# The bias of a graph network's C projection in 64x64 tiles, and a new order of the period

## The chip, the cores and the metric

The kernel runs on one core of one Trainium2 chip. The core has five engines that work side by side, each with an instruction queue of its own that it executes in order: PE (TensorE, matmuls), DVE (VectorE), ACT (ScalarE), POOL (GpSimd) and SP (which only issues DMAs here). The metric is the device time of one execution in microseconds (us). Before the change three runs took 699.24, 699.70 and 699.98 us; the median is 699.7.

## What is computed

There are 128 graphs of 128 nodes with 64 features (x), each with a dense 128x128 matrix adj, about 6% of it nonzero. Two layers follow each other, each with a residual and a normalisation over the features.

```python
# layer 0, per graph: mask = adj > 0
h   = relu((x @ W1a)[j] + (x[j] - x[k]) @ W1b + b1)    # for every pair j, k; 192 wide
hm  = sum over k of h * mask[j, k]
x   = layernorm(x + hm @ W2 + deg[j] * b2)             # deg[j] = number of neighbours of j
# layer 1, per graph
agg = adj @ x
out = elu(elu(agg @ V1 + c1) @ V2 + c2) @ V3 + c3
x   = layernorm(x + out)
```

The pair sum is not computed densely. For each node j the kernel gathers only the rows of its neighbours: h[j, k] = relu(A[j] + C[k]) with A = x @ (W1a + W1b) + b1 and C = -x @ W1b. The sum of relu is taken from the sum of absolute values, since relu(t) = (t + |t|) / 2, and the linear half is put right by a correction (corr). The term deg[j] * b2 comes for free if every neighbour's row of C carries b2 in 64 extra columns: C has 192 + 64 = 256 columns, and the last 64 are multiplied by the mask itself, not by the relu.

## The kernel before

**Work.** Two graphs make a pair; there are 64 pairs, and the steady state is one pair per period. In a pair the nodes are sorted by degree and laid into nine blocks (BLOCKS), each with a number of neighbour slots. Block i of a pair is a "unit": ACT copies A into a PSUM bank (L955, here called acopy i), PE adds the neighbours' C rows by 18 matmuls against one-hot matrices (L966, gather i), and DVE sums absolute values over the slots (L976, sum i). Three PSUM banks (e0 to e2) rotate among the units, so acopy of a unit waits for the sum of the unit three before it. C is held as three bf16 parts (cf, rest, low) whose sum is the f32 value; each gather takes all three.

**The threads of a pair.** prepare counts degrees (mk, L576), spreads them on PE (L263, tiles identb and degb), ranks them (cmp, L597) and makes the permutation (perm, L605). sort_x sorts x, projects A (L632, L636), makes aj and later ea, sa and corr. sort_mask sorts the mask and makes the nine one-hot matrices (oh, L707). turn transposes adj and x. project_c makes C (L741), adds the bias in a step of its own, and splits the result. finish makes hm, multiplies by W2, returns to the node order (unsort), normalises, and does layer 1 (aggregate, hidden1, hidden2, last), up to the store. Five more PSUM banks (m0 to m4) serve all these steps; a step takes the bank that was given back first, and so waits for whoever read it last.

**The bias before.** b2 is split into three bf16 parts too. A 128x64 tile b2p is zero except in rows 0, 32 and 64, which hold the parts (copied there by POOL, L393), so that a matmul of a 128-row matrix of ones with b2p adds the sum of the parts to every row. The step is named bias in project_c, with 128x64 tiles (mode "t"), between the projection in 64x64 tiles (mode "r", L741) and the copy cf (L756).

**Order.** Nothing is ordered by hardware waits alone. A small planner (class Flow) writes the instructions into the queues. Every thread is a list of steps, each with an engine, a planned cost and the events it needs, and DUE gives each step a due time relative to its pair's start, ROUND (11.1651) apart. Until the first gather is laid, the planner takes the step that its planned clocks say is ready first. From then on (under_way) it takes, of all steps whose inputs are laid already, the one with the smallest due time. LAST shifts the dues of the last six pairs' finish threads, and pairs from LATE = NP - 2 on do more of finish on DVE and ACT. The overflow test (L858 to L879) near the end finds rows with too many neighbours for their block; none are found for these inputs, and a slow path behind it isn't run.

**Constants.** consts_b2 loads and splits b2 on POOL (helper parts, L389 to L393); scratch tiles hi, hm (as rest), mid and low are shared with the later split of c3's row (consts_late). consts_slots, on POOL, ends with memsets, one of them for b2p.

Of the kernel before, what the change touches and what calls it, by code (L numbers as in the profile page):

```python
# [31 lines left out]
F32 = mybir.dt.float32  # L32
# [3 lines left out]
OP = mybir.AluOpType  # L36
# [150 lines left out]
def sparse(tc, env):  # L187

    g = type("env", (), dict(env))
    nc, P, N, F, H, O, HB, H1, NP, E = (  # L190
        g.nc, g.P, g.N, g.F, g.H, g.O, g.HB, g.H1, g.NP, g.E)
# [11 lines left out]
    AHEAD = 4  # L203

    DUE = {
        "prepare": (-21.4113, -21.4103, -20.8009, -20.0167, -16.5154),
        "sort_x": (-11.5423, -11.5413, -2.7266, -2.3845, 0.0214, 1.3277, 2.8168, 12.6347),
        "sort_mask": (-10.347, -9.218, -8.7754, -8.3524, -5.8935, -5.758, -5.757, -5.756,
            -5.755, -5.754, -5.1217, -5.1207, 1.0998, 1.1008),
        "turn": (-26.2816, -24.1632),  # L210
        "project_c": (-13.6709, -12.5698, -12.2977, -12.2751, -11.3882, -10.0036, -8.4866),
        "finish": (13.0404, 22.189, 23.0263, 23.6287, 24.5439, 27.278, 28.4137, 32.117, 34.5413,
            35.4475, 35.4637, 36.1308, 36.1318, 36.1328, 37.7091, 43.35, 43.6764, 45.3519,
            45.5256, 46.0637, 48.8402, 49.096, 49.261, 51.6959, 51.9284),
        "unit": [(-1.48, -0.1838, 0.7496), (0.1062, 0.9216, 0.9226), (0.3987, 1.0968, 1.978),
            (1.1956, 1.4908, 2.221), (2.1682, 2.6234, 3.9141), (2.1874, 3.6496, 4.2699),
            (2.4467, 4.3465, 5.2271), (8.5772, 9.7062, 10.187), (5.7368, 9.4611, 10.7836)],
        "consts_late": (14.79, 24.13, 25.63, 26.63, 26.78, 26.79, 26.8, 26.81, 26.82, 27.82,
            28.82, 29.82, 30.82, 31.82, 32.82, 33.82, 34.82, 35.82, 36.82, 37.82, 38.82, 39.82,
            40.82),  # L220
    }

    LATE = NP - 2
    LAST = ((-3.5, -9.4, -4.9, -1.3), (5.5, -4.3, 0.3, 7.6), (-0.9, -2.8, 3.8, 7.6), (0.1, -0.2, -0.4, 5.1), (0.0, -1.6, 0.0, 0.2), (0.0, 0.0, 0.2, 0.0))

    def begin_thread(name, p, gen):
        due = DUE[name]
# [30 lines left out]
    HALVES = (slice(0, P // 2), slice(P // 2, P))  # L258

    def tiled(out, lhsT, rhs, **kw):  # L260

        for h in HALVES:
            nc.tensor.matmul(out[h], lhsT[:, h], rhs, **kw)  # L263
# [9 lines left out]
    const, temp = g.const, g.const  # L273
# [12 lines left out]
    ident = const([P, P], F32, "ident")  # L286
    identb = const([P, P], BF16, "identb")
    onesb = const([P, 2 * P], BF16, "onesb")
# [19 lines left out]
    wc = const([P, H + O], F32, "wc")  # L308
# [10 lines left out]

    b2r = const([P, O], F32, "b2r")  # L320
    b2p = const([P, O], BF16, "b2p")
    NR = 2 * O
    rows = temp([P, NR], F32, "rows")
    rowp = const([P, NR], BF16, "rowp")
# [15 lines left out]
    def made(*names):  # L340
        return [event("const", name) for name in names]

    def op(engine, cost, fn, name, *after):

        ev, = yield (engine, cost, made(*after), 0, fn)
        happened(ev, "const", name)
# [39 lines left out]
    def parts(row, to, n):  # L386

        hi, rest, mid, low = (t[:, :n] for t in scratch)
        return [("hi", lambda e: e.tensor_copy(hi, row)),  # L389
                ("rest", lambda e: e.tensor_sub(rest, row, hi)),  # L390
                ("mid", lambda e: e.tensor_copy(mid, rest)),
                ("low", lambda e: e.tensor_sub(low, rest, mid))] + [
                    (f"{i}", lambda e, i=i, t=t: e.tensor_copy(to[32 * i:32 * i + 1, :],  # L393
                                                               t[32 * i:32 * i + 1, :]))
                    for i, t in enumerate((hi, mid, low))]
# [18 lines left out]
    def consts_slots():  # L414
        v = nc.gpsimd
        iota = dict(allow_small_or_imprecise_dtypes=True)
        for i, (base, n, p0, p1, s) in enumerate(LAY):
            yield from op("POOL", 0.45, lambda: v.iota(
                slotc[:, base:base + n], pattern=[[2, s], [0, p1 - p0]], base=1,
                channel_multiplier=0, **iota), "slotc" if i == NB - 1 else f"slotc{i}")  # L420

        def scale():
            for p0, p1, s in BLOCKS:
                v.memset(srow[:, :, p0:p1], float(s))
        yield from op("POOL", 1.0, scale, "srow")
        yield from op("POOL", 0.2, lambda: v.memset(b2p, 0.0), "b2p0")
        for s in range(2):
            yield from op("POOL", 0.3, lambda: v.memset(v1p[:, s], 0.0), f"v1p0{s}")

# [64 lines left out]
        yield from op("DVE", 0.3, blocks, "wad", "wa", "wab0")  # L494

    def consts_b2():
        last = ["b2", "b2p0"]
        for name, fn in parts(b2r, b2p, O):
            yield from op("POOL", 0.25, lambda: fn(nc.gpsimd), "b2" + name, *last)
            last = ["b2" + name]  # L500
        happened(event("const", "b22"), "const", "b2p")

    def consts_banks():

# [227 lines left out]
    def project_c(p, ev):  # L732

        d = S[p]
        cols = H + O

        def project(*cps):
            for s in range(2):
                k = slice(s * F, (s + 1) * F)
                for h in HALVES:  # L740
                    nc.tensor.matmul(cps[s][h, :cols], d["turned"][k, 2, h], wc[k, :],  # L741
                                     start=True, stop=False)
        ev, *cps = yield ("PE:r", 0.43, [ev] + made("wc"), 2, project)

        def bias():
            for s in range(2):
                tiled(cps[s][:, H:cols], onesb[:, :P], b2p, start=False, stop=True)
        ev, = yield ("PE:t", 0.06, [ev] + made("b2p", "onesb"), 0, bias)
        cf = prep.tile([P, 2, cols], F32, name="cf", bufs=6)
        rest = prep.tile([P, 2, cols], F32, name="rest", bufs=6)  # L750
        low = prep.tile([P, 2, cols], BF16, name="low", bufs=6)
        d["cp"] = lambda i, s, c: low[:, s, c] if i == 2 else upper((cf, rest)[i][:, s, :])[:, c]
        hi = []
        for s in range(2):
            e, = yield ("ACT", act(cols), [ev], 0,
                        lambda: nc.scalar.copy(cf[:, s, :], cps[s][:, :cols]))  # L756
            hi.append(e)
        for s in range(2):
            ev, = yield ("DVE", dve(cols), [hi[s]], 0,
                         lambda: nc.vector.tensor_sub(rest[:, s, :], cps[s][:, :cols],  # L760
                                                      upper(cf[:, s, :])))
            flow.give(cps[s], ev)
        ev, = yield ("POOL PORT", 1.12, [ev], 0,
                     lambda: nc.gpsimd.tensor_sub(flat(low), flat(rest), upper(flat(rest))))  # L764
        happened(ev, "cp", p)
# [468 lines left out]
```

## Time and profile before

| | us |
|---|---|
| median of three runs | 699.7 (699.24 to 699.98) |
| the profiled execution itself | 699.37 |
| its span, first to last instruction | 697.6 |
| PE busy | 676.6 (97%) |
| DVE busy | 674.2 (97%) |
| ACT busy | 621.2 (89%) |
| POOL busy | 583.4 (84%) |
| gathers, L966, three groups | 210.9, 209.0, 209.0 |
| sums, L976 | 336.8 |
| one-hot compares, L707 | 155.9 |

A busy share counts the time in which the engine has at least one instruction under way; PE's matmuls overlap and their ends are modelled, so for PE the distance from one start to the next says more than the duration. In timeline lines the first number is the start in us after the span's start, the second the duration of all that the line merges ("x4": four instructions), then engine, line of the kernel, operation, output<-inputs by tile names, and shapes. PEld is the weight load of PE. In the groups, a number after the bar is busy time and mean ns of one. Windows give each engine's busy time in a stretch, then the granted clock of PE, the DMA share and GB/s.

### The profile page before, as it was taken

To read this page: it belongs to the slowest core of one execution; us is meant where nothing else is said; L and a number is where in the kernel's file an instruction comes from. 1 tells how busy PE (TensorE), PEld (TensorE's weight loads), DVE (VectorE), ACT (ScalarE), POOL (GpSimd) and SP (SyncE) were. 2 spreads that over 40 slices of the span, in tenths; PEclk is the share of its full clock that TensorE was granted. 3 is DMA by queue.
4 is the path that set the end of the run, shared out by engine and by line. 5 is a ranking of instruction groups with operands and counts; after the bars stand their busy time and mean duration, and the time that the engine had idled before them with its cause. 6 is when DMAs were issued, how large, how long until landed. Compare 5 with 4: busy or idle time off the path is not lost.

```text
span 697.6 us, 40860 instructions
## 1 busy us (share of the span) xinstructions
PE 676.6 (97%) x17245; PEld 610.3 (87%) x17246; DVE 674.2 (97%) x2267; ACT 621.2 (89%) x1731; POOL 583.4 (84%) x983
## 2 busy tenths in 40 slices
PE   7989999999999999999999999999999999999984
PEld 4878999999999999999999999999999999989972
DVE  6899999999999999999999999999999999999985
ACT  3678999999999999999999999999999999999963
POOL 5447988988988898898899889899888888899873
PEclk9999999999999999999999999999999999999996
DMA  3200111110110111111011011101101101100000
GB/s 93 56 3 3 35 26 27 35 34 19 34 34 19 33 34 26 27 34 34 19 35 33 23 31 34 32 20 34 34 19 33 34 23 30 35 22 9 12 9 20
DMA packets 54988, 20.01 MB, mean 29 GB/s; under 512 B 37904, under 2 KB 54800, under 8 KB 54800
## 3 DMA queue, kind: packets, MB, share of 16 engines
q1 hardware_dynamic: 54096, 17.06, 10.1%
q8 instruction: 137, 2.24, 1.3%
q14 instruction: 51, 0.42, 0.2%
q10 hardware_dynamic: 704, 0.30, 0.2%
HBM read 13.14 MB, written 4.19 MB: 25 GB/s over the span
## 4 chain that ended last, share of the span: by engine, by line
PE 90%; DVE 4%; POOL 2%; ACT 2%; issue 1%; DMA 1%; SPq 0%; POOLq 0%; DVEq 0%; ACTq 0%
PE e L966 46%; PE m L263 23%; PE m L741 4%; PE m L636 3%; PE m L722 3%; PE m L917 2%; PE m L619 2%; PE m L632 2%; DVE sums L976 1%; PE m L657 1%; PE m L661 1%; PE m L723 1%; POOL rs L787 1%; ACT e L955 1%; DVE oh L707 1%
## 5 line engine op out<-in xcount | busy, mean ns | idle before, releaser
L955 ACT COPY e<-aj 128x504 f32<-128x504 f32 (+6 forms) x576 | 311.3, 551 | 39.1 <-DVE sums L976 36.9
L976 DVE TENSOR_REDUCE sums<-e 128x54 f32<-128x486 f32 (+8 forms) x576 | 336.8, 603 | 3.5 <-PE e L966 2.1
L966 PE MATMUL e<-oh,cf 128*64 128x162 bf16 (+6 forms) x3456 | 210.9, 229 | 4.3 <-ACT e L955 4.0
L966 PE MATMUL e<-oh,rest 128*64 128x162 bf16 (+6 forms) x3456 | 209.0, 227 | 0.0
L966 PE MATMUL e<-oh,low 128*64 128x162 bf16 (+6 forms) x3456 | 209.0, 227 | 0.0
L966 PEld LDWEIGHTS <-cf 128*64 128x64 bf16 x3456 | 150.3, 110 | 30.7 <-issue 29.8
L707 DVE TENSOR_TENSOR oh<-vp,slotc 128x336 bf16<-128x336 bf16 (+6 forms) x576 | 155.9, 325 | 0.3 <-ACT vp L700 0.3
L966 PEld LDWEIGHTS <-rest 128*64 128x64 bf16 x3456 | 141.4, 110 | 0.0
L966 PEld LDWEIGHTS <-low 128*64 128x64 bf16 x3456 | 141.1, 110 | 0.3 <-POOL low L764 0.3
L841 POOL TENSOR_TENSOR h<-up,e 128x256 f32<-128x256 f32 x124 | 95.9, 774 | 10.4 <-ACT up L839 10.3
L787 POOL TENSOR_TENSOR rs<-ve,mhalf 128x2 f32<-128x2 f32 x128 | 92.0, 719 | 13.9 <-DVE ve L784 3.5
L764 POOL TENSOR_TENSOR low<-rest 128x512 bf16<-128x512 f32 x64 | 66.6, 1040 | 9.8 <-DVE rest L760 9.8
L651 POOL TENSOR_TENSOR sa<-aj,srow 128x384 f32<-128x384 f32 x64 | 65.6, 1025 | 8.1 <-DVE perm L605 4.0
L889 POOL TENSOR_TENSOR hm<-sums,corr 128x384 f32<-128x384 f32 x62 | 62.3, 1005 | 4.9
L674 POOL TENSOR_TENSOR corr<-ea,sa 128x384 f32<-128x384 f32 x64 | 65.3, 1020 | 0.0
L831 ACT ACTIVATE r<-m,cc 128x256 f32<-128x256 f32 x128 | 61.8, 483 | 3.5 <-PE m L263 3.3
L839 ACT ACTIVATE up<-m,cc 128x256 f32<-128x256 f32 x124 | 58.0, 468 | 0.0
L834 ACT ACTIVATE e<-r 128x256 f32<-128x256 f32 x128 | 53.4, 417 | 2.2
L760 DVE TENSOR_TENSOR rest<-m,cf 128x256 f32<-128x256 f32 x128 | 51.9, 407 | 0.0
L784 POOL TENSOR_SCALAR ve<-st 128x2 f32<-128x2 f32 x124 | 33.6, 271 | 20.5 <-DVE st L777 9.6
L756 ACT COPY cf<-m 128x256 f32<-128x256 f32 x128 | 41.4, 377 | 7.2 <-PE m L263 5.5
L643 ACT ACTIVATE aj<-m,b1n 128x128 f32<-128x128 f32 x128 | 40.0, 364 | 3.7 <-PE m L636 2.2
(163 smaller groups left out, 1459.4 us busy)
## 6 DMA issues: line engine op xcount, KB each, us to landing
adj<-in_adj_dram SPq DMA_DIRECT2D x64, 128.0 KB, 2.5
xx<-in_x_dram SPq DMA_DIRECT2D x64, 64.0 KB, 2.2
out_dram<-o SPq DMA_DIRECT2D x64, 64.0 KB, 1.7
w1s<-in_L_gnn_W_dram ACTq DMA_DIRECT2D x2, 96.0 KB, 2.9
w2s<-in_L_gnn_W_dram ACTq DMA_DIRECT2D x2, 48.0 KB, 2.5
v2s<-in_L_gnn_W_dram SPq DMA_DIRECT2D x1, 64.0 KB, 2.1
v1d<-in_L_gnn_W_dram SPq DMA_DIRECT2D x2, 32.0 KB, 2.0
rows<-in_L_gnn_b_dram SPq DMA_DIRECT2D x1, 64.0 KB, 5.5
```

The lines of the kernel that those rows point to most:

```text
L263: nc.tensor.matmul(out[h], lhsT[:, h], rhs, **kw)
L651: evs, = yield ("POOL PORT", 1.0, [have] + made("srow"), 0, lambda: nc.gpsimd.tensor_mul(sa, aj, srow))
L674: ev, = yield ("POOL PORT", 1.05, [ev, evs], 0, lambda: nc.gpsimd.tensor_sub(corr, ea, sa))
L707: lambda: nc.vector.tensor_tensor(oh[:, 2 * base:2 * (base + n)].rearrange("p (b s w) -> p b s w", b=2, w=w), vp[:, :, p0:p1].rearrange("p ...
L764: lambda: nc.gpsimd.tensor_sub(flat(low), flat(rest), upper(flat(rest))))
L787: nc.gpsimd.tensor_tensor(rs, ve, mhalf, op=OP.pow)
L831: lambda: nc.scalar.activation(r, z, AF.Relu, bias=c, scale=-1.0))
L841: ev, = yield ("POOL PORT", 0.64, [ev, evr], 0, lambda: nc.gpsimd.tensor_add(h, up, e))
L889: lambda: (nc.vector if late else nc.gpsimd).tensor_sub(hm, d["sums"], d["corr"]))
L955: lambda: nc.scalar.copy(e.rearrange("p (c s w) -> p c s w", c=3, w=w), d["aj"][:, :, p0:p1].rearrange("p c (o w) -> p c o w", o=1) .to_br ...
L966: nc.tensor.matmul(e[HALVES[h], c * n:(c + 1) * n], cp(k, s, slice(chunk * HB, (chunk + 1) * HB)), oh[:, 2 * base + s * n:2 * base + (s + ...
L976: nc.vector.tensor_reduce(d["sums"][:, :, p0:p1], e.rearrange("p (c s w) -> p c w s", c=3, w=w), AX.X, OP.add, apply_absolute_value=True)
```

## The change

The bias of C is no longer a step of its own. Its four matmuls stand in the projection's step, with 64x64 tiles: each graph s uses 64 rows of ones (its own partition half) against the same half of b2p. So b2p must hold the three parts in both halves. It is built by masks: third[:, k] is 1 in rows k and 64 + k (from two slices of the identity), and b2p becomes the sum over k of part k times third[:, k], in four DVE instructions instead of a memset and three row copies on POOL. The projection step now needs b2p and the ones too, and its planned cost is 0.47 instead of 0.43 plus 0.06. All due times (DUE) and the shifts of the last pairs (LAST) are new; ROUND, BLOCKS and the costs of the other steps stay.

```diff
     DUE = {
-        "prepare": (-21.4113, -21.4103, -20.8009, -20.0167, -16.5154),
-        "sort_x": (-11.5423, -11.5413, -2.7266, -2.3845, 0.0214, 1.3277, 2.8168, 12.6347),
-        "sort_mask": (-10.347, -9.218, -8.7754, -8.3524, -5.8935, -5.758, -5.757, -5.756,
-            -5.755, -5.754, -5.1217, -5.1207, 1.0998, 1.1008),
-        "turn": (-26.2816, -24.1632),
-        "project_c": (-13.6709, -12.5698, -12.2977, -12.2751, -11.3882, -10.0036, -8.4866),
-        "finish": (13.0404, 22.189, 23.0263, 23.6287, 24.5439, 27.278, 28.4137, 32.117, 34.5413,
-            35.4475, 35.4637, 36.1308, 36.1318, 36.1328, 37.7091, 43.35, 43.6764, 45.3519,
-            45.5256, 46.0637, 48.8402, 49.096, 49.261, 51.6959, 51.9284),
-        "unit": [(-1.48, -0.1838, 0.7496), (0.1062, 0.9216, 0.9226), (0.3987, 1.0968, 1.978),
-            (1.1956, 1.4908, 2.221), (2.1682, 2.6234, 3.9141), (2.1874, 3.6496, 4.2699),
-            (2.4467, 4.3465, 5.2271), (8.5772, 9.7062, 10.187), (5.7368, 9.4611, 10.7836)],
...
+        "prepare": (-25.3269, -24.5959, -16.2313, -15.6835, -13.6455),
+        "sort_x": (-10.9448, -7.4273, -1.9926, -1.7844, 2.4124, 11.797, 13.4753, 13.4763),
+        "sort_mask": (-8.5308, -7.4543, -6.624, -5.5003, -3.1373, -2.6816, -2.6806, -2.6796,
+            -2.6786, -2.6776, -2.4981, -2.4971, -2.4961, -2.4951),
+        "turn": (-25.244, -24.172),
+        "project_c": (-13.1291, -12.8893, -10.6576, -9.7608, -9.0798, -9.0501),
+        "finish": (16.813, 21.0899, 22.6525, 22.736, 25.343, 29.1235, 31.0649, 33.1532, 37.5085,
+            38.243, 39.6553, 41.5238, 41.7347, 41.7545, 41.7555, 42.911, 43.5062, 43.7424,
+            43.8552, 45.7261, 49.7417, 50.8421, 51.2192, 54.4516, 54.4526),
+        "unit": [(-1.48, -0.0856, 1.4248), (0.9695, 2.41, 2.411), (1.0649, 2.7067, 4.0064),
+            (3.4417, 4.152, 4.3887), (4.8199, 6.203, 7.8143), (4.9295, 6.3829, 7.9158), (4.9634,
+            8.0955, 8.4797), (8.528, 9.3261, 9.6798), (8.5344, 9.7003, 11.9339)],
...
-    LAST = ((-3.5, -9.4, -4.9, -1.3), (5.5, -4.3, 0.3, 7.6), (-0.9, -2.8, 3.8, 7.6), (0.1, -0.2, -0.4, 5.1), (0.0, -1.6, 0.0, 0.2), (0.0, 0.0, 0.2, 0.0))
+    LAST = ((-2.5, -8.6, -10.0, -8.0), (4.1, -0.3, 0.0, 0.0), (0.0, -1.8, 0.5, 4.7), (0.4, 1.6, 0.0, 3.8), (0.0, -0.1, -0.0, -0.0), (-0.0, 0.0, -0.2, 0.6))
...
+    third = const([P, 3], F32, "third")
...
-        yield from op("POOL", 0.2, lambda: v.memset(b2p, 0.0), "b2p0")
...
     def consts_b2():
-        last = ["b2", "b2p0"]
-        for name, fn in parts(b2r, b2p, O):
+        last = ["b2"]
+        for name, fn in parts(b2r, b2p, O)[:4]:
             yield from op("POOL", 0.25, lambda: fn(nc.gpsimd), "b2" + name, *last)
             last = ["b2" + name]
-        happened(event("const", "b22"), "const", "b2p")
+        hi, mid, low = (scratch[i][:, :O] for i in (0, 2, 3))
+
+        def place(v):
+            v.tensor_add(third, ident[:, 0:3], ident[:, HB:HB + 3])
+            v.tensor_scalar(b2p, hi, third[:, 0:1], None, op0=OP.mult)
+            for k, t in ((1, mid), (2, low)):
+                v.scalar_tensor_tensor(b2p, t, third[:, k:k + 1], b2p, op0=OP.mult, op1=OP.add)
+        yield from op("DVE", 0.6, lambda: place(nc.vector), "b2p", "ident", *last)
...
-        ev, *cps = yield ("PE:r", 0.43, [ev] + made("wc"), 2, project)
-
-        def bias():
-            for s in range(2):
-                tiled(cps[s][:, H:cols], onesb[:, :P], b2p, start=False, stop=True)
-        ev, = yield ("PE:t", 0.06, [ev] + made("b2p", "onesb"), 0, bias)
+            for s in range(2):
+                k = slice(s * F, (s + 1) * F)
+                for h in HALVES:
+                    nc.tensor.matmul(cps[s][h, H:cols], onesb[k, :HB], b2p[k, :],
+                                     start=False, stop=True)
+        ev, *cps = yield ("PE:r", 0.47, [ev] + made("wc", "b2p", "onesb"), 2, project)
```

The due times of consts_late (late constants, in the first periods) are new too: its second step moves from 24.13 to 28.66 and its last from 40.82 to 43.74.

More of the change, by code (lines that the diff above doesn't have):

```diff
@@ L215, in sparse @@
-        "unit": [(-1.48, -0.1838, 0.7496), (0.1062, 0.9216, 0.9226), (0.3987, 1.0968, 1.978),
-            (1.1956, 1.4908, 2.221), (2.1682, 2.6234, 3.9141), (2.1874, 3.6496, 4.2699),
-            (2.4467, 4.3465, 5.2271), (8.5772, 9.7062, 10.187), (5.7368, 9.4611, 10.7836)],
-        "consts_late": (14.79, 24.13, 25.63, 26.63, 26.78, 26.79, 26.8, 26.81, 26.82, 27.82,
-            28.82, 29.82, 30.82, 31.82, 32.82, 33.82, 34.82, 35.82, 36.82, 37.82, 38.82, 39.82,
-            40.82),
+        "prepare": (-25.3269, -24.5959, -16.2313, -15.6835, -13.6455),
@@ L221, in sparse @@
+        "unit": [(-1.48, -0.0856, 1.4248), (0.9695, 2.41, 2.411), (1.0649, 2.7067, 4.0064),
+            (3.4417, 4.152, 4.3887), (4.8199, 6.203, 7.8143), (4.9295, 6.3829, 7.9158), (4.9634,
+            8.0955, 8.4797), (8.528, 9.3261, 9.6798), (8.5344, 9.7003, 11.9339)],
+        "consts_late": (13.69, 28.66, 30.16, 31.16, 31.31, 31.32, 31.33, 31.34, 31.35, 32.35,
+            33.22, 34.1, 34.98, 35.85, 36.73, 37.61, 38.48, 39.36, 40.24, 41.11, 41.99, 42.87,
+            43.74),
     }
     LATE = NP - 2
-    LAST = ((-3.5, -9.4, -4.9, -1.3), (5.5, -4.3, 0.3, 7.6), (-0.9, -2.8, 3.8, 7.6), (0.1, -0.2, -0.4, 5.1), (0.0, -1.6, 0.0, 0.2), (0.0, 0.0, 0.2, 0.0))
+    LAST = ((-2.5, -8.6, -10.0, -8.0), (4.1, -0.3, 0.0, 0.0), (0.0, -1.8, 0.5, 4.7), (0.4, 1.6, 0.0, 3.8), (0.0, -0.1, -0.0, -0.0), (-0.0, 0.0, -0.2, 0.6))
```

## The prediction

> **What bounds the kernel now.** I read the page first (engine shares, chain of waits), then the steady stretch by windows, then one quiet and one late period on the timeline, then the start and the tail.
>
> ```profile
> PE 676.6 (97%) x17245; PEld 610.3 (87%) x17246; DVE 674.2 (97%) x2267; ACT 621.2 (89%) x1731; POOL 583.4 (84%) x983
> ...
> PE 90%; DVE 4%; POOL 2%; ACT 2%; issue 1%; DMA 1%; SPq 0%; POOLq 0%; DVEq 0%; ACTq 0%
> ```
> ```profile
> 300.00:400.00 100.00, 100.00 (x2614) 91.47 (x2610) 99.66 (x332) 94.08 (x264) 89.11 (x147) 1.00 0.12 28
> ```
> TensorE (PE) and VectorE (DVE) are both full; the granted clock there is 1.00. The chain lies on PE, but DVE is only a hair behind, so PE alone can't be asked. A pair of graphs takes one period. From one copy of xsT to the next, the last 57 periods of the trace last 10.245 us in the mean: 45 of them 10.20 to 10.21, twelve 10.32 to 10.55. The excess of these over 10.205 is 2.3 us in all. PE's starts are the same to a few ns from period to period, so 10.205 is PE's own work. The twelve late periods are explained by two stretches, a quiet one and a late one:
>
> ```profile
> 319.43 0.27 DVE L576 TENSOR_SCALAR_CACHE_REDUCE mk<-adj 128x128 bf16<-128x128 f32 x1
> 320.12 0.56 DVE L707 TENSOR_TENSOR oh<-vp,slotc 128x308 bf16<-128x308 bf16 x2
> 320.44 0.83 POOL L841 TENSOR_TENSOR h<-up,e 128x256 f32<-128x256 f32 x1
> 320.61 0.40 DVE L760 TENSOR_TENSOR rest<-m,cf 128x256 f32<-128x256 f32 x1
> ...
> 329.55 0.27 DVE L576 TENSOR_SCALAR_CACHE_REDUCE mk<-adj 128x128 bf16<-128x128 f32 x1
> 330.27 1.12 DVE L707 TENSOR_TENSOR oh<-vp,slotc 128x308 bf16<-128x308 bf16 x2
> 330.38 0.81 POOL L841 TENSOR_TENSOR h<-up,e 128x256 f32<-128x256 f32 x1
> 331.32 0.40 DVE L760 TENSOR_TENSOR rest<-m,cf 128x256 f32<-128x256 f32 x1
> ```
> ```profile
> 321.40 0.28 PE L263 MATMUL m<-identb,degb 128*64 128x128 bf16 x4
> ...
> 331.78 0.30 PE L263 MATMUL m<-identb,degb 128*64 128x128 bf16 x4
> ```
> DVE's period is mk to mk: 329.55 - 319.43 = 10.12 us, 0.085 below PE's. So DVE gains on PE each period until its two one-hot compares (oh, L707) meet POOL's h, which then started first: the pair of compares takes 1.12 instead of 0.56, rest comes 0.55 late, and the degree spread on PE, whose bank of PSUM this rest gives back, starts 0.17 late (10.38 after the last one). Then it begins again. So: floor PE 10.205, DVE 10.12, about one late period in five.
>
> **Part 1, the bias.** Removed: a step of its own, four 128x64 matmuls.
> ```profile
> 345.95 0.61 PE L741 MATMUL m<-wc,turned 64*64 64x256 f32 x8
> ...
> 347.79 0.22 PE L263 MATMUL m<-b2p,onesb 128*64 128x64 bf16 x4
> 347.85 0.63 PE L263 MATMUL m<-h,v2s 128*64 128x256 f32 x4
> ```
> From its start to the next matmul's start it occupies PE for 0.058 us (347.79 to 347.85). Added: four 64x64 matmuls of the same 64 columns at the end of L741's step. Four tiles of L741 start 6 to 7 ns apart and run side by side, whereas the two halves of a 128x64 step come in pairs (the bias's two pairs 0.028 apart). So the four new ones are one pass of about 0.029 instead of two: saving 0.029 a period, 57 x 0.029 = 1.7 us. The Trainium skill, "TensorEngine Tiling (Array Packing)", Instruction Overhead, speaks against it: a matmul has about 60 cycles of overhead, and no tiling factor should be taken from a dimension that is small already. If the four paid those one after the other (some 25 ns each, an estimate from the page), the step would cost 0.10, 0.042 more than now: +2.4 us. I take the row, since L741's tiles overlap. Bounds: +2.4 to -1.7. Entries to and exits from 64x64 tiles stay one per period, because turn (due 8.25 within the period), project_a (9.17) and project_c (9.20) are still neighbours. cf needs no later step any more; it waited 0.1 to 0.2 for the bias in 26 of 49 periods, on ACT, which has 6% to spare: nothing.
>
> **Part 2, the order.** Once the first gather is issued, the smallest due time goes first, so each engine's queue is the table sorted modulo 11.1651; the table of before, sorted so, gives the timeline's order. PE after (g = gather): g8, W2, g0, sort_x, unsort, short, g1, sort_mask, g2, aggregate, g3, last, prefix, spread, hidden1, g4, g5, g6, turn, project_a, project_c with bias, g7, hidden2. No PE work is added, so I lay it end to end with the start-to-start times of the steady timeline: g8 ends at 0.67, g0 1.94, unsort 2.39, short 2.71, g1 3.0, sort_mask 3.23, g2 3.88, aggregate 4.13, g3 4.57, last 4.86, spread 5.08, hidden1 5.52, g4 6.17, g5 6.77, g6 7.54, turn 7.92, project_a 8.51, project_c 9.08, g7 9.71, hidden2 10.175. A result is readable about 0.2 later (bias 347.79 + 0.22, cf at 348.04).
>
> DVE after: sum8, rest0, sum0, rest1, ea, sum1, y1, sum2, sum3, y2, st2, rank, st1, sum4, sum5, mk, sum6, all nine oh, permute, sum7. Same instructions, 10.12 to 10.13. Laid against PE, sum3 ends the wait last: sum8 starts at 1.41 or later (sum3 is 3.36 further on and needs g3 at 4.77). Then rest0 ends at 2.34 and rest1 at 3.24, and the steps that reuse their banks come at 3.00 (sort_mask) and 3.88 (aggregate): about 0.45 to spare once 0.15 of hand-over is counted. Before, rest1 ended at 341.84 and the spread started at 342.01: none. The spread now takes the bank of xsT, free for 1 us. ACT: acopy2 waits for sum8 (2.0), runs to 2.7, g2 wants it at 3.23; acopy4 ends at 5.0 behind agg, g4 at 5.52; all others have more. So PE waits for nobody, with 0.35 the smallest slack, and the 2.3 us of late periods go. On SP, the load of a later pair goes out with sum6, now at 8.48 instead of 5.23 in the period; it lands after 2.5 (the page) and is read more than a period later. The store goes behind oscale, and only loads stand after it: nothing.
>
> POOL after: var2, oscale, x1scale, h2, low, corr, sa, hm, h1, var1, degb/keyc. h1 now ends around 8.15 (up1 7.3, hm 7.33) and the compares begin at 8.57: the collision of before has 0.4 of room. In exchange ten DVE instructions with two SBUF inputs stand in one run of 2.43 us. The Trainium skill, "SBUF — State Buffer", Who interferes with whom, says that such an instruction and a GpSimd one that reads SBUF block each other for a whole instruction, whichever is first. If POOL were shut out for the whole run, its period would be its 8.9 to 9.1 busy plus 2.4, over 11: +0.9 us a period. The row: in the run of eight now (2.0 us) ve takes 0.33 instead of 0.19 in 46 of 49 cases, rs its usual 0.70 in 40 and 1.0 in 6; one ve of 49 took 1.40. I take 0.5 for degb, keyc and two ve, so POOL needs 9.5 of 10.18 and is hidden; if that cover is gone, low is late for g0.
>
> **Part 3, start and end.** The first project_c now needs b2p, so its place in PE's queue is behind b2p.
> ```profile
> 10.88 0.30 POOL L392 TENSOR_TENSOR low<-hm,mid 128x64 bf16<-128x64 f32 x1
> 11.10 1.13 PE L741 MATMUL m<-wc,turned 64*64 64x256 f32 x8
> 15.74 0.32 PE L263 MATMUL m<-b2p,onesb 128*64 128x64 bf16 x4
> 18.25 1.04 POOL L764 TENSOR_TENSOR low<-rest 128x512 bf16<-128x512 f32 x1 [6.06 <-DVE rest L760]
> 18.30 0.62 PE L966 MATMUL e<-oh,cf 128*64 128x162 bf16 x6
> ```
> POOL's three row copies and a memset go; DVE gets four small ops (third, and three of 128x64; 0.07 to 0.3 each by the neighbours, 0.6 in all) in the 2.86 us in which it now sits idle before 14.08. b2p is then there near 11.9, project_c starts 0.8 later than at 11.10, but its bias does not come at 15.74: cf and rest can run before 15.4, ahead of the compares, and the first gather needs only those. Room: 18.30 - 16.6 = 1.7 at most, 2.3 if DVE's idle (2.86 and 1.58 later) is all used; at worst +0.9, if everything behind project_c is late by its delay. I take -1.0, nearer the gain.
>
> Tail: ea(63) moves behind the last sum8, so corr on POOL (1.0) and hm follow it: +0.4 (0.1 + 1.0 + 0.1 + 0.55 + 0.47 of ea, less the 0.47 that sum8 gains and the 1.31 in which hm ended after sum8). The overflow test's hit and bad move behind h1 of the last pair, which now starts at 686.13 although its e ended at 685.4: -0.7. Near nothing; bounds +1.5, -1.5.
>
> **Sum.** Profiled execution 699.4 (span 697.6 and 1.8 around it), 0.3 under the median of 699.7. Median 699.7 - 1.7 (bias) - 2.3 (late periods) - 1.0 (start) + 0 (tail) = 694.7, say 694.8. A measurement of this kernel tells about 0.2% (1.4 us) from no change.
>
> **Rivals.**
> (A) The forecast, 692.5 to 697.8: 0.55.
> (B) DVE stays the pace. For: 10.12 is only 0.055 below the new PE floor, so one lost 0.5 us in nine periods eats it all; other compares may meet oscale or x1scale. Then the period stays at 10.24, and start and bias give 1 to 1.5: 697.8 to 701.1, likeliest 699. Against: 0.45 of slack takes up one such loss. 0.22, half of it within 0.2%.
> (C) Slower: POOL in the single run of compares. If each ran on as the one ve of 1.40 did, POOL passes 10.18 when it loses over 1.1 us a period; at 1.4 lost the period is about 10.4, 57 x 0.16 = +9 us on the present: 708. Against: 46 of 49. 0.15.
> (D) The bias or start doesn't do what it says (serial tiles, +2.4; project_c's wait at the head of PE's queue, +0.9) and the late periods go only in part: 700 to 703. 0.08.
> Faster 0.66 (A, half of B), same 0.13 (B, a part of D), slower 0.21 (C, most of D). Range: 692.3 to 704, cutting the faster end of A and the far half of C; A alone 692.5 to 697.8.
>
> **What would show it.** Right: starts of project_c to the next gather 0.57 instead of 0.541 and no b2p row of 128x64; nearly all periods 10.17 to 10.18; no compare above 0.45; first gather near 17. Wrong: PE waiting for DVE in the wait list, or ve, degb, keyc, oscale stretched and low or x1scale awaited by PE; a period over 10.2 with compares stretched; or a gather behind turn/project_c with a longer exit.

## The result, and the profile after

The changed kernel takes **694.08 us** (median of four runs, 693.39 to 694.43), the kernel before on the same chip 699.47: a ratio of 0.9922, 95% interval 0.9904 to 0.9939. The forecast was 694.8, range 692.3 to 704.0. The total is met, but the parts are not: two gains were larger than forecast, and a loss of 4.0 us near the start is missing from the forecast's sum.

The profiled execution took 693.39 us, its span is 691.6. The page of the kernel after, engine shares and chain of waits:

```profile
PE 665.8 (96%) x17245; PEld 608.0 (88%) x17246; DVE 668.3 (97%) x2271; ACT 627.3 (91%) x1731; POOL 583.4 (84%) x979
...
PE 91%; DVE 4%; ACT 2%; DMA 1%; issue 1%; SPq 0%; POOL 0%; POOLq 0%; DVEq 0%; ACTq 0%
```

The steady stretch by windows (busy us and instructions of PE, PEld, DVE, ACT, POOL; then granted clock, DMA share, GB/s):

```profile
300.00:400.00 100.00, 100.00 (x2652) 92.38 (x2648) 99.66 (x339) 96.55 (x270) 90.61 (x149) 1.00 0.12 30
```

Shares say little here: PE and DVE are as full as before. The counts say more. In the same 100 us PE issues 2652 matmuls instead of 2614, 1.5% more.

The steady period on PE, kernel after (start, duration, engine, line, operation):

```profile
340.89 0.38 PE L924 MATMUL m<-turned,x 128*64 128x128 f32 x4
341.11 0.31 PE L973 MATMUL e<-oh,cf 128*64 128x112 bf16 x6
...
345.50 0.61 PE L748 MATMUL m<-wc,turned 64*64 64x256 f32 x8
345.93 0.21 PE L753 MATMUL m<-b2p,onesb 64*64 64x64 bf16 x4
346.07 0.39 PE L973 MATMUL e<-oh,cf 128*64 128x154 bf16 x6
...
346.70 0.59 PE L263 MATMUL m<-h,v2s 128*64 128x256 f32 x4
347.13 0.39 PE L973 MATMUL e<-oh,cf 128*64 128x170 bf16 x6
```

and the same steps of the kernel before:

```profile
340.11 0.42 PE L917 MATMUL m<-turned,x 128*64 128x128 f32 x4
340.36 0.39 PE L966 MATMUL e<-oh,cf 128*64 128x168 bf16 x6
...
346.49 0.41 PE L966 MATMUL e<-oh,cf 128*64 128x170 bf16 x6
...
348.31 0.38 PE L619 MATMUL m<-perm,xx 128*64 128x128 f32 x4
```

Read the starts. The projection with its bias takes 346.07 - 345.50 = 0.57 until the next gather starts (before, without the bias, 346.49 - 345.95 = 0.54). hidden2 (h,v2s) takes 0.43; before, behind the bias step, it took 348.31 - 347.85 = 0.46. aggregate (turned,x) takes 0.22; before it took 340.36 - 340.11 = 0.25.

The one-hot compares of the kernel after, DVE with POOL beside them:

```profile
314.42 0.73 POOL L848 TENSOR_TENSOR h<-up,e 128x256 f32<-128x256 f32 x1 [0.17 <-ACT up L846]
314.43 0.28 DVE L583 TENSOR_SCALAR_CACHE_REDUCE mk<-adj 128x128 bf16<-128x128 f32 x1
...
315.43 2.15 DVE L714 TENSOR_TENSOR oh<-vp,slotc 128x324 bf16<-128x324 bf16 x9
315.50 0.81 POOL L794 TENSOR_TENSOR rs<-ve,mhalf 128x2 f32<-128x2 f32 x1
316.27 0.37 POOL L590 CAST degb<-degs 128x2 bf16<-128x2 f32 x1
316.60 0.28 POOL L591 TENSOR_TENSOR keyc<-degs,jcol 128x2 f32<-128x2 f32 x1
...
324.54 0.28 DVE L583 TENSOR_SCALAR_CACHE_REDUCE mk<-adj 128x128 bf16<-128x128 f32 x1
```

h ends at 315.15, before the compares begin. Nine compares take 2.15 us (0.24 each): none is held up. POOL pays instead: degb takes 0.37, where 0.18 was usual before. DVE's period is 324.54 - 314.43 = 10.11.

Where the time went, by the starts of the gather of block 0 of each pair in the two traces:

| stage | before, us | after, us | difference |
|---|---|---|---|
| span's start to first gather | 18.30 | 16.91 | -1.39 |
| first gather to that of the third pair | 19.13 | 19.53 | +0.40 |
| third to sixth pair (late constants) | 34.60 | 38.64 | **+4.04** |
| sixth to ninth pair | 30.62 | 30.37 | -0.25 |
| the next 52 periods | 532.79 | 526.50 | **-6.29** |
| last three periods | 30.22 | 29.27 | -0.95 |
| last pair's gathers | 9.90 | 8.33 | -1.57 |
| behind the last gather | 22.05 | 22.00 | -0.05 |

Over the 52 periods the mean is 10.125 instead of 10.246. They are nearly all alike: the usual one is 10.124, and only one differs visibly (10.18).

### The profile page after: what moved, and what is told of

Same layout as the page of the kernel before. It is cut to its first block, busy times and chain, and to the rows that moved or that the text cites. A ratio compares the mean times of both kernels' runs of the same rounds, so it can differ in the third digit from the quotient of the medians.

```text
span 691.6 us, 40984 instructions
## 1 busy us (share of the span) xinstructions
PE 665.8 (96%) x17245; PEld 608.0 (88%) x17246; DVE 668.3 (97%) x2271; ACT 627.3 (91%) x1731; POOL 583.4 (84%) x979
## 4 chain that ended last, share of the span: by engine, by line
PE 91%; DVE 4%; ACT 2%; DMA 1%; issue 1%; SPq 0%; POOL 0%; POOLq 0%; DVEq 0%; ACTq 0%
PE e L973 48%; PE m L263 22%; PE m L748 4%; PE m L643 3%; PE m L729 3%; PE m L639 2%; PE m L924 2%; PE m L626 2%; PE m L664 1%; DVE oh L714 1%; DVE sums L983 1%; PE m L730 1%; PE m L668 1%; ACT e L962 1%; PE m L670 1%
## 5 line engine op out<-in xcount | busy, mean ns | idle before, releaser
L983 DVE TENSOR_REDUCE sums<-e 128x54 f32<-128x486 f32 (+8 forms) x576 | 332.9, 603 | 4.9 <-PE e L973 2.9
L962 ACT COPY e<-aj 128x504 f32<-128x504 f32 (+6 forms) x576 | 303.5, 547 | 29.0 <-DVE sums L983 28.2
L973 PEld LDWEIGHTS <-cf 128*64 128x64 bf16 x3456 | 145.5, 111 | 31.7 <-issue 20.1
L714 DVE TENSOR_TENSOR oh<-vp,slotc 128x336 bf16<-128x336 bf16 (+6 forms) x576 | 139.2, 314 | 0.0
L794 POOL TENSOR_TENSOR rs<-ve,mhalf 128x2 f32<-128x2 f32 x128 | 107.4, 839 | 14.0 <-DVE ve L791 3.7
L848 POOL TENSOR_TENSOR h<-up,e 128x256 f32<-128x256 f32 x124 | 90.6, 731 | 12.8 <-ACT up L846 11.0
L838 ACT ACTIVATE r<-m,cc 128x256 f32<-128x256 f32 x128 | 63.3, 494 | 4.9 <-PE m L263 4.0
L841 ACT ACTIVATE e<-r 128x256 f32<-128x256 f32 x128 | 53.4, 418 | 4.2
L846 ACT ACTIVATE up<-m,cc 128x256 f32<-128x256 f32 x124 | 56.6, 457 | 0.0
L763 ACT COPY cf<-m 128x256 f32<-128x256 f32 x128 | 49.5, 387 | 3.0 <-PE m L753 3.0
L748 PE MATMUL m<-wc,turned 64*64 64x256 f32 x512 | 40.1, 378 | 2.9 <-DVE rows L550 2.8
```

Source lines behind the costliest of these rows:

```text
L714: lambda: nc.vector.tensor_tensor(oh[:, 2 * base:2 * (base + n)].rearrange("p (b s w) -> p b s w", b=2, w=w), vp[:, :, p0:p1].rearrange("p ...
L794: nc.gpsimd.tensor_tensor(rs, ve, mhalf, op=OP.pow)
L838: lambda: nc.scalar.activation(r, z, AF.Relu, bias=c, scale=-1.0))
L848: ev, = yield ("POOL PORT", 0.64, [ev, evr], 0, lambda: nc.gpsimd.tensor_add(h, up, e))
L962: lambda: nc.scalar.copy(e.rearrange("p (c s w) -> p c s w", c=3, w=w), d["aj"][:, :, p0:p1].rearrange("p c (o w) -> p c o w", o=1) .to_br ...
L973: nc.tensor.matmul(e[HALVES[h], c * n:(c + 1) * n], cp(k, s, slice(chunk * HB, (chunk + 1) * HB)), oh[:, 2 * base + s * n:2 * base + (s + ...
```

## Experiments

Every kernel below computes the full result. "Usual period" is the one from which the late periods stand out. "Pair 8" is the start of the gather of block 0 of the ninth pair (numbered from 0), 102.66 us before and 105.45 after. Each trace is one execution, and its first microseconds vary: with the same start, the first gather came at 18.30, 18.41 and 18.66 in three traces with the old order and the old bias, and at 16.78, 16.96 and 18.07 in three with the old order and the new bias.

### Which part brings it: the bias alone, the order alone

**The bias alone:** the kernel before, with the tiles of the new bias step and the new b2p, the due times kept.

```diff
-        "project_c": (-13.6709, -12.5698, -12.2977, -12.2751, -11.3882, -10.0036, -8.4866),
+        "project_c": (-13.6709, -12.2977, -12.2751, -11.3882, -10.0036, -8.4866),
...
-        ev, = yield ("PE:t", 0.06, [ev] + made("b2p", "onesb"), 0, bias)
+                    nc.tensor.matmul(cps[s][h, H:cols], onesb[k, :HB], b2p[k, :],
+                                     start=False, stop=True)
+        ev, *cps = yield ("PE:r", 0.47, [ev] + made("wc", "b2p", "onesb"), 2, project)
```

> The old order with only the bias moved into project_c's step (its own due time dropped, b2p built by masks). Forecast's theory: the new order removes the late periods, the bias only one pass of 0.029 us. Then PE's period falls from 10.205 to 10.176, the collisions of the one-hot compares with POOL's h stay, and the time is 699.5 - 1.7 or so = 697.8. Rival, from the profile after (hidden2 takes 0.431 there instead of 0.462): an f32 step that follows a step of short matmuls costs 0.03 more, so that dropping the bias step is worth 0.06 a period; then hidden2 shows 0.43, undisturbed periods 10.145, and the time is 699.5 - 3.4 - up to 1.4 at the start = 694.7 to 696.1. Second rival: VectorE is the pace, period stays at 10.24, time 698 to 699.5.

**The order alone:** the kernel after, with all its due times, but with the old b2p and the bias as a step of its own again, in the place that it had before, ahead of hidden2.

```diff
-        "project_c": (-13.1291, -12.8893, -10.6576, -9.7608, -9.0798, -9.0501),
+        "project_c": (-13.1291, -12.93, -12.8893, -10.6576, -9.7608, -9.0798, -9.0501),
```

> The new order with the old bias step: four 128x64 matmuls, laid directly ahead of hidden2 (due -12.93), b2p by row copies. Forecast's theory: 0.029 more a period than after, 10.138, 694.1 + 1.7 = 695.8. Rival (an f32 step behind short matmuls costs 0.03): hidden2 shows 0.46, period 10.169, 694.1 + 3.4 = 697.5. If VectorE is the pace at 10.109, both are partly hidden: under 695.

**The order alone, the bias step near:** the same, with the step right behind the projection (due -13.128 instead of -12.93).

> As the run before, but the old bias step is laid directly behind project_c (due -13.128), ahead of the gather of block 7, so hidden2 follows a gather. Forecast's theory and the rival agree on the bias (0.058 instead of 0.029), the rival adds nothing for hidden2: period 10.138 to 10.14, 694.1 + 1.7 = 695.8. Against the run before: the same by the forecast's theory, 1.7 us faster by the rival.

| | time, us | ratio to before, 95% | usual period | mean of 52 periods | pair 8 |
|---|---|---|---|---|---|
| before | 699.98 | | 10.205 | 10.246 | 102.66 |
| bias alone | 695.03 | 0.9931 (0.9915 to 0.9947) | 10.148 | 10.166 | 103.83 |
| order alone | 699.80 | 1.0005 (0.9995 to 1.0015) | 10.186 | 10.186 | 106.58 |
| order alone, near | 697.34 | 0.9972 (0.9961 to 0.9983) | 10.160 | 10.161 | 105.89 |
| after | 694.08 | 0.9922 (0.9904 to 0.9939) | 10.124 | 10.125 | 105.45 |

The row of the kernel after is from the result above; the others were measured together. The bias is worth 10.205 - 10.148 = 0.057 in the old order and 10.186 - 10.124 = 0.062 in the new one, twice the 0.029 of the forecast: in the run of the bias alone the rival holds, in period and time. The order alone shortens the mean period by 0.060, but reaches pair 8 3.9 us later, and ends with nothing gained. So the bias alone brings nearly the whole gain of the change (ratio 0.9931 against 0.9922; the intervals overlap). Both runs of the order alone are slower than either side expected, by 2.3 and 1.5 us; 1.1 and 0.4 of it, against the kernel after, are lost before pair 8.

Why twice? The timeline of PE in the two runs of the order alone; first the run with the bias step ahead of hidden2:

```profile
349.20 0.23 PE L263 MATMUL m<-b2p,onesb 128*64 128x64 bf16 x4
349.26 0.63 PE L263 MATMUL m<-h,v2s 128*64 128x256 f32 x4
349.72 0.39 PE L966 MATMUL e<-oh,cf 128*64 128x170 bf16 x6
```

and the run with the step near the projection:

```profile
347.31 0.25 PE L263 MATMUL m<-b2p,onesb 128*64 128x64 bf16 x4
347.39 0.37 PE L966 MATMUL e<-oh,cf 128*64 128x154 bf16 x6
...
348.00 0.59 PE L263 MATMUL m<-h,v2s 128*64 128x256 f32 x4
348.43 0.39 PE L966 MATMUL e<-oh,cf 128*64 128x170 bf16 x6
```

The very same hidden2 takes 0.46 behind the four short bias matmuls and 0.43 behind a gather. So the old bias step cost its own 0.058 and 0.03 more in the step behind it, 0.088 in all; the new one costs 0.57 - 0.54, some 0.03. The difference, 0.06, is the 0.057 to 0.062 measured. Against the run with the step near, where hidden2 is not touched, the new tiles bring 10.160 - 10.124 = 0.036: that is the saving which the forecast had counted as 0.029. (In that run the bias step takes 0.08 and the gather behind it 0.61; with the new tiles the bias adds 0.03 and the gather takes 0.63. So what stands right behind the 64x64 tiles takes some 0.02 longer, and 0.69 - 0.66 = 0.03 is the difference.)

### What lowers PE's floor in the new order

aggregate had the same 0.03: 0.25 us behind the gather of block 1 (66 columns) in the kernel before, 0.22 behind one of 168 columns after. **One due time moved** puts it there in the old order too:

```diff
-        "finish": (..., 32.117, 34.5413,
+        "finish": (..., 32.117, 34.6,
```

> The kernel before, with aggregate (f32, four matmuls of 128 columns) laid behind the gather of block 2 (168 columns) instead of that of block 1 (66 columns): due 34.5413 becomes 34.6. Theory of the f32 step behind short matmuls: from its start to the next start 0.217 instead of 0.247, PE's period 10.175, 1.5 to 1.7 us faster. Rival: the 0.03 belongs to what follows or to the clock, aggregate stays at 0.247 and the time is the same.

Measured: 698.87 us, ratio 0.9985 (0.9977 to 0.9993), a gain of 1.1 us by the ratio where 1.5 to 1.7 were expected. aggregate takes 0.22, the usual period is 10.18 instead of 10.205, the late periods stay (about one in six, 10.39 with 10.22 behind it). **Both together**, the new bias step and this one due time, everything else as before:

> The old order with the new bias step, and one due time moved (finish's ninth, 34.5413 to 34.6), so that aggregate stands behind a gather of 168 columns instead of one of 66. Theory (an f32 step right behind short matmuls costs about 0.03 more, and nothing else of the new order counts in the steady state): start of bias-carrying period 10.148 - 0.03 = 10.12 as in the changed kernel, with the few late periods of the bias-alone run left; time 695.0 - 57 x 0.03 = about 693.4. Rival (the new order as a whole is needed for 10.124): period stays at 10.148, time 695.

Measured: 693.22 us, ratio 0.9889 (0.9873 to 0.9906); usual period 10.121, mean 10.130, pair 8 at 104.01. The timeline of PE in that run:

```profile
349.34 0.39 PE L924 MATMUL m<-turned,x 128*64 128x128 f32 x4
349.56 0.40 PE L263 MATMUL m<-ys,permT 128*64 128x64 f32 x8
```

aggregate takes 0.22 here too, and the expectation is met. So the old order with two edits has the floor of the new one. The rest of the new table of due times is not needed for it.

### The late periods, and which engine is the pace

**rest1 ahead of the compares.** The forecast put the late periods down to a PSUM bank that the second rest gives back late. Here that rest goes ahead of the two compares, in the kernel before:

```diff
-        "project_c": (-13.6709, -12.5698, -12.2977, -12.2751, -11.3882, -10.0036, -8.4866),
+        "project_c": (-13.6709, -12.5698, -12.2977, -12.2751, -11.3882, -10.075, -8.4866),
```

> The kernel before, with the second rest subtraction of a pair laid ahead of the two one-hot compares that can meet POOL's h (due -10.0036 becomes -10.075), so that the bank for the degree spread is given back before a collision. Forecast's theory: the late periods come from that bank; they vanish, PE's period is 10.205 throughout, and the time falls by 2.0 to 2.3 us, 699.5 to 700 becoming 697.3 to 698. Rival: the lost half microsecond of VectorE only shows at its next consumer, late periods stay, same time.

Measured: **766.07 us**, ratio 1.0922 (1.0880 to 1.0964): the expectation failed. The timeline of this run:

```profile
340.76 0.42 DVE L760 TENSOR_TENSOR rest<-m,cf 128x256 f32<-128x256 f32 x1
340.93 0.73 POOL L841 TENSOR_TENSOR h<-up,e 128x256 f32<-128x256 f32 x1
341.10 1.81 DVE L707 TENSOR_TENSOR oh<-vp,slotc 128x308 bf16<-128x308 bf16 x2
341.62 1.07 POOL L674 TENSOR_TENSOR corr<-ea,sa 128x384 f32<-128x384 f32 x1
```

The two compares now begin behind h's start in 45 of 46 periods and take 1.81 us together instead of 0.56: by their own rows 0.74 and 1.15, so that the first ends 0.18 behind h and the second 0.22 behind corr. The spread on PE no longer waits for that bank, and yet the period is 11.36: now everything behind the compares is late, ACT's copies by up to 1.5 us for the sums (75.3 us of waiting in 500), prefix on PE by 0.6 for y. So what is lost here is DVE's time in the collision itself. The bank is not tested by itself, since the same edit moved the compares: in the kernel before, one compare of a pair waits (0.87 instead of about 0.3) in about one period of five; here both wait in nearly every one. The Trainium skill, "SBUF — State Buffer", Who interferes with whom, has the rule (a DVE operation with two SBUF inputs and a GpSimd one that reads SBUF exclude each other for a whole instruction), and the order of starts here agrees with it: each compare waits out one POOL instruction. DVE's share from 300 to 400 us is 99.7% in this run: time blocked counts as busy.

**More work for DVE.** Is DVE still the pace, with 10.11 of 10.124 us? The kernel after, with a memset of 64 columns that nobody reads in each pair:

```diff
+    junk = const([P, O], F32, "junk")
...
+            nc.vector.memset(junk, 0.0)
```

> The changed kernel with one more VectorE instruction per pair (a memset of 128x64 f32 to a tile that nobody reads, about 0.1 us). If VectorE has next to no room (its undisturbed period 10.11 against PE's 10.124), the period rises to about 10.2 and the time by 4 to 5 us, to 698 to 699. If PE alone is the pace with room to spare, it stays at 694.

Measured: 694.89 us, ratio 0.9915 (0.9899 to 0.9932). The timeline of DVE:

```profile
347.79 0.09 DVE L584 DVE_READ_ACCUMULATOR mk<-adj 128x1 f32 x1
347.84 0.11 DVE L586 MEMSET junk<- 128x64 f32 x1
347.86 0.63 DVE L985 TENSOR_REDUCE sums<-e 128x39 f32<-128x507 f32 x1
348.40 2.15 DVE L716 TENSOR_TENSOR oh<-vp,slotc 128x324 bf16<-128x324 bf16 x9
```

The usual period stays 10.125 (10.124 without the memset). From sum to compares it is now 0.54 instead of 0.60 us: the memset takes 0.06 that DVE had been waiting inside an instruction which the profile calls busy. PE alone is the pace, and the rival in which DVE keeps it falls. (In this trace pair 8 comes 2.2 us later, at 107.67. It has one more stretch at half clock, from 22.7 to 26.1 us, and its first gather is 0.6 late; the steady period is not touched.)

### The loss at the start

The late constants (consts_late) are worked out once, between the gathers of the third and the sixth pair. PE around 47 us in the kernel after:

```profile
42.57 0.28 PE L541 MATMUL m<-onesf,v2s 128*128 128x1 f32 x2
...
43.61 0.60 PE L748 MATMUL m<-wc,turned 64*64 64x256 f32 x4
47.01 0.43 PE L748 MATMUL m<-wc,turned 64*64 64x256 f32 x2 [2.80 <-DVE rows L550]
```

and DVE in the same stretch:

```profile
43.42 2.55 DVE L714 TENSOR_TENSOR oh<-vp,slotc 128x324 bf16<-128x324 bf16 x9
...
46.74 0.21 DVE L550 TENSOR_TENSOR rows<-rows,m 128x64 f32<-128x64 f32 x1
```

The late constants' matmul (L541) now stands between turn and project_a and takes one of the five banks. Its reader on DVE stands behind the nine compares, so the second half of project_c waits 2.80 us for that bank. What comes next is seen in the windows of the same kernel, the third number from the end being the granted clock:

```profile
46.00:48.50 2.50, 1.49 (x34) 1.19 (x36) 0.89 (x6) 0.78 (x2) 0.00 (x0) 1.00 0.00 0
48.50:52.00 3.50, 3.50 (x63) 3.50 (x61) 2.21 (x7) 1.35 (x5) 0.00 (x0) 0.52 0.02 5
52.00:54.00 2.00, 2.00 (x66) 1.96 (x66) 2.00 (x8) 1.15 (x4) 0.91 (x1) 0.99 0.00 0
```

From 48.6 to 52.0 PE is granted half its clock, and 3.4 us at half clock are up to 1.7 us of matmuls lost. Both runs of the order alone and the run with the memset have such a gap and show the same stretch behind it (3.4 us at 0.50, between 47 and 53.4); the kernel before and the bias alone have neither. The Trainium skill, "TensorE: Matmul & The Clock Gate", Part 1, says that PE falls to half clock after about 3.4 us of idleness and is watched in windows of this length; the length agrees, but here a gap of 2.80 us (2.67 in the runs of the order alone) was followed by it. Even a gap of 1.53 us was, with rest1 ahead of the compares (half clock from 20.4) and with aggregate moved (from 17.2), and one of 1.56 in the run with the memset; in the kernel after, one of 1.55 us at 19.0 was not. What trips it is not shown.

**The late constants three us earlier** (all due times of consts_late but the first, in the kernel after):

```diff
-        "consts_late": (13.69, 28.66, 30.16, ..., 43.74),
+        "consts_late": (13.69, 25.66, 27.16, ..., 40.74),
```

> The changed kernel with all due times of the late constants but the first 3 us earlier, so that their matmul does not hold a PSUM bank while turn, project_a and project_c take the other five. Theory: project_c's wait of 2.8 us for the tile rows on VectorE (at 44 to 47 us), and the slow clock behind it, are the loss of the start; the wait goes and the time falls by 2.5 to 4.5 us, to 689.6 to 691.6, with the steady period unchanged at 10.11. Rival: the start is bound by VectorE's own extra work (late constants 3.7 to 5.3 us), so only the place changes: 693.5 to 694.5.

Measured: 693.16 us, ratio 0.9919 (0.9895 to 0.9943), where the kernel after has 0.9922: the time of 689.6 to 691.6 was missed, and no gain is clear of noise. In the trace, which is of the fastest of the four runs (691.93; the other three have a lower mean granted clock, 0.986 to 0.989 against 0.993), pair 8 is at 103.38, 2.07 earlier. The wait of 2.80 is gone and the clock stays at 1.00 there. Third to sixth pair is now 36.58 instead of 38.64, still above the 34.60 of before, with one period of 14.29. In that one DVE splits the row of c3 (helper parts), and its operations take longer than on POOL in the next run:

```profile
53.54 0.82 DVE L390 CAST mid<-hm 128x128 bf16<-128x128 f32 x1
55.29 1.05 DVE L391 TENSOR_TENSOR low<-hm,mid 128x128 bf16<-128x128 f32 x1
```

**The split on POOL as well:**

```diff
-            yield from op("DVE", 0.4, lambda: fn(nc.vector), "row" + name, *last)
+            yield from op("POOL", 0.4, lambda: fn(nc.gpsimd), "row" + name, *last)
```

> The kernel with the late constants 3 us earlier (693.2), and also the split of c3's row into three bf16 parts (seven instructions, 3.3 us with their stretching) on POOL instead of VectorE; POOL sits idle for 8 us there. If the start is bound by VectorE, its loss goes: 1.5 to 3 us faster, 690.2 to 691.7. If something else is late in the start (PE's clock after a wait, a bank), the time stays at 693.

Measured: **690.96 us**, ratio 0.9867 (0.9846 to 0.9887), pair 8 at 102.07, usual period 10.125. The same two operations in this run:

```profile
55.95 0.29 POOL L390 CAST mid<-hm 128x128 bf16<-128x128 f32 x1
56.32 0.43 POOL L391 TENSOR_TENSOR low<-hm,mid 128x128 bf16<-128x128 f32 x1
```

Third to sixth pair takes 34.85, so 3.79 of the 4.04 us are back. This version beats both kernels. **The old order with the same ideas** (new bias step, aggregate's due time, split on POOL):

> The same with the row split of the late constants on POOL instead of DVE. Theory (late constants delay the first periods through DVE whatever the order): the eighth pair's first gather comes 1.3 us or more earlier than in the bias-alone run (103.83), time about 691 to 692. Rival (that gain depends on the new order; in the old one POOL's split meets the compares): no earlier than 103.8 and 693.4 or more.

Measured: 691.95 us, ratio 0.9866 (0.9848 to 0.9885), pair 8 at 103.16. The time is as the theory says, the place is not: pair 8 is 0.7 earlier than with the bias alone, not 1.3. From the third to the sixth pair it takes 32.68 instead of 34.58, but in this trace the first gather comes at 18.07. So the split on POOL saves as much in the old order (1.9 us) as in the new one (1.73): it is a gain of its own. With the split in the same place, the new order still takes 2.0 to 2.2 us more from the third to the sixth pair (36.58 against 34.55, 34.85 against 32.68), and what makes this rest is not shown. Against the kernel before on the same chip it gains as much as the version above, without the new table.

## Why the prediction was right, and where it was not

**What bounds the kernel: right.** PE's work sets the period; all 52 periods but one are PE's floor. DVE at 10.11 is just below it, and the memset shows that it has still a little to give. Rivals A and B are told apart: A it is.

**Part 1, the bias: right mechanism, half the size.** The forecast's step was one pass instead of two, 0.029 a period, -1.7 us. The tiles did that (0.036 with the step near; 0.57 from the projection to the next gather, the figure named as the sign). What it left out is the neighbour: hidden2 behind the short bias matmuls took 0.03 more, and loses that when the step goes. Together 0.057 to 0.062, over 55 periods 3.1 to 3.4 us. The overhead per matmul that was weighed against the row is not seen: the four tiles cost 0.03 together, not 0.10.

**Part 2, the order: the late periods go, as forecast, and a shorter floor alone thins them out too.** They were to bring 2.3 us; the excess over the usual period was 0.041 in the mean (10.246 - 10.205), over 52 periods 2.1, and is gone. The run of the order alone shows that the order does it. From 100 to 620 us it has no compare above 0.35, although PE's floor is still 10.186; the kernel before has eleven of 0.64 to 0.88 there, one for each late period. Yet the bias alone, in the old order, has only four late periods of 52, with four compares of 0.62 to 0.65, and with aggregate moved as well two such compares; before it was about one period in five. That fits the forecast's own picture: DVE gains on PE by the difference of the two periods until compares and h meet. With 10.205 against 10.12 it gains 0.085 a period; with 10.148 only about 0.03. The nearer PE's floor is to DVE's, the rarer the meeting. Whether the bank of the second rest is what passes a late compare on stays open: freeing it moved the compares behind h for good, 66 us slower, and so tested something else. The floor, said to be 10.17 to 10.18, came to 10.124: in laying the new sequence end to end with the old step times, the 0.03 of aggregate and the 0.03 of hidden2 were overlooked.

**POOL: right that it is hidden, too dear in size.** The forecast took 0.5 us a period as lost to the run of ten. rs rose from a median of 0.70 to 0.83 and degb from 0.18 to 0.37, but keyc fell from 0.35 to 0.28, and both ve of a pair take 0.19, where one took 0.33 before. POOL's busy time in a period went from 9.11 to 9.15 us, 0.04 more. No compare of the steady state takes above 0.35. POOL is hidden, so rival C falls.

**Part 3, the start: the step that failed.** Its end came about, its times did not. b2p was ready at 13.58, not near 11.9, and the first project_c came at 14.08, 3.0 later than before instead of 0.8. Yet its bias follows at once, cf and rest run ahead of the compares as described, and the gather is near 17:

```profile
13.30 0.28 DVE L507 SCALAR_TENSOR_TENSOR b2p<-low,third,b2p 128x64 bf16<-128x64 bf16 x1 [0.26 <-DVE b2p L507]
...
14.08 0.80 PE L748 MATMUL m<-wc,turned 64*64 64x256 f32 x8
...
14.72 0.20 PE L753 MATMUL m<-b2p,onesb 64*64 64x64 bf16 x4
...
16.91 0.41 PE L973 MATMUL e<-oh,cf 128*64 128x162 bf16 x6 [0.48 <-ACT e L962]
```

The first gather is 1.39 earlier, and at the third pair 0.99 are left: the -1.0 of the sum. But that agreement is luck, because those 0.99 are not the bias's: the two runs of the order alone, with the old bias, have their third pair at 36.98 and 36.39, as early as the kernel after (36.44). And the part ended there. The moved steps of consts_late stood in the change (28.66 for 24.13), and the forecast gave them no cost. From the third to the sixth pair 4.04 us are lost; 2.06 of them go when these steps alone move back by 3 us. They were a matmul that takes a bank ahead of project_c, a reader behind nine compares, and the half clock behind the gap. The rest of the 4.04 stays open. The rule that was passed over is that of every moved step: what it occupies until its reader comes.

That an earlier start needn't count was also not seen. With the bias alone the first gather is at 16.78, but the third pair comes at 38.81 instead of 37.43. The windows between the two, of the bias alone:

```profile
16.78:38.81 22.03, 17.41 (x411) 14.53 (x409) 21.39 (x54) 14.28 (x38) 8.35 (x8) 1.00 0.19 49
```

and the compares of these pairs, with POOL beside the first ones:

```profile
17.43 3.06 DVE L714 TENSOR_TENSOR oh<-vp,slotc 128x132 bf16<-128x132 bf16 x6
17.59 1.21 POOL L771 TENSOR_TENSOR low<-rest 128x512 bf16<-128x512 f32 x1 [3.69 <-DVE rest L767]
18.77 1.05 POOL L658 TENSOR_TENSOR sa<-aj,srow 128x384 f32<-128x384 f32 x1
...
27.52 2.21 DVE L714 TENSOR_TENSOR oh<-vp,slotc 128x308 bf16<-128x308 bf16 x2
```

There DVE is busy for 21.39 of 22.03 us and PE for 17.41 only, so in the first two periods DVE sets the pace. With the earlier start the compares of these pairs stand beside POOL's low, sa and corr, and four of them take 1.12 to 1.16 us instead of about 0.3. It is the collision of the steady state in another place, 3.3 us in all, more than the 1.5 by which the first gather is early.

**Tail: right in these two traces.** 22.05 became 22.00. Other traces of the old order have 20.4 to 22.0 us there, those of the new one 22.0 to 22.8, so a difference of 1 us is not excluded. The last pairs gain 2.5 us more (0.95 and 1.57), which the forecast had not looked at. The 1.57 come with the new due times and LAST, not with the bias: the last pair's gathers take 8.49 and 8.50 in the runs of the order alone, 10.15 with the bias alone. How much of that is LAST and how much the order wasn't tried.

**The sum.** Forecast -1.7 - 2.3 - 1.0 + 0 = -5.0. Measured in the spans: -0.99 (start), +4.04 (late constants), -6.55 (the 55 periods from the sixth pair on), -2.52 (the last pairs), -0.05 (tail), together -6.1; the medians differ by 5.4. The forecast met the total because what it missed nearly cancels: 4.0 us lost between the third and the sixth pair against 2.5 won at the end and 2.5 more than forecast in the periods. That is luck. The mechanism was right for the period, and there two sizes were off.

## What to carry to other kernels

A step's price on TensorE is not its own start-to-start time alone: look at what the step behind it takes there and elsewhere, and put short matmuls ahead of a step that takes no longer behind them. A moved step is costed with the buffer it holds until its reader has run, and once-only work at the start counts like the steady loop: here the stretch with the late constants ate two thirds of what 52 periods gained. When two engines are nearly level, shortening the slower one also thins out the collisions that come from the faster one running ahead.

## What the runs showed of the hardware

- An f32 step of four matmuls right behind short bf16 matmuls takes 0.03 us longer: hidden2 0.46 against 0.43, aggregate 0.25 against 0.22, each seen in two or more kernels with only its neighbour changed. Why is not shown.
- A compare that starts while POOL's h or corr runs ends 0.2 us behind it: a pair took 1.81 instead of 0.56 us, in nearly every period, and the kernel 66 us more. The time counts as busy.
- A gap of 2.67 to 2.80 us on TensorE around 47 us was followed within 1.6 us by 3.4 us at half clock (granted 0.50), in all four traces that have it. Behind gaps of about 1.5 us half clock came in some traces and not in others.
